# Attention over 26 causal tiles: all early projections first, and the seven shortest tiles set between longer ones

## The chip, the cores and the metric

The kernel runs on one core of a Trainium2 chip. A core has a matrix engine (PE, with its weight loads shown apart as PEld), a vector engine (DVE), a scalar engine (ACT), a general engine (POOL) and a queue engine (SP) that issues transfers here. Each works through its own instructions in the order in which they were written; semaphores join them. The metric is the time of one execution on the device in microseconds (us).

## What is computed

Two layers of a graph network on 3327 nodes with 256 features. Layer 0 is a normalised graph convolution and a mixture of 8 experts, layer 1 a graph attention and a last feed-forward block. Only that last block (`_L1_ffn_ref`) is touched. Cut to what matters:

```python
sx = einsum('bsh,ndh->bnsd', x, hl_w) + hl_b          # x: layer-normed rows; 4 heads of 64
q = einsum('bnsd,neod->bneso', sx, wq)                # 4 experts for each head
k = einsum('bnsd,nod->bnso', sx, wk)
v = einsum('bnsd,nod->bnso', sx, wv)
scores = einsum('bnesd,bntd->bnest', q, k) * d ** 0.5 + causal
att = softmax(scores, axis=-1)
qkv = einsum('bnest,bntd->bnesd', att, v)             # zero where sx is zero
# a softmax gate mixes the 4 experts; + residual; layernorm; two small
# linear layers; layernorm; a softmax gate over the heads; + x
```

The causal mask makes the work of a row grow with its place: row s attends to rows 0 to s.

## The kernel before

`heads` (line 745) does this block. The rows lie in 26 tiles of 128. A unit is a tile t and a head h; its keys are cut into chunks of 512 columns, so that a unit has t // 4 + 1 chunks and the last one has 128, 256, 384 or 512 columns. In all there are 392 chunks, from 4 in each of tiles 0 to 3 up to 28 in tiles 24 and 25.

`prepare(t)` (line 852) makes what a tile needs: it loads the rows `xres` from the DRAM tensor `xs`, normalises them (`pst`, `pmv`, `prs` with a power on POOL, `xn`), turns them on PE (`xt`), projects them (`psxt`, evicted to `sxt`), copies them by four transfers to the layout `sxd`, makes the values (`pv`, `v`, four stores to the DRAM tensor `vs`), the keys (`pk`, into `kt`, which holds the keys of all tiles), the queries (`pq`, `qt`), a zero mask in `sxd` and the turned rows `sx`. It is a Python generator of nine steps: each `yield` lets other work be written in between. `begin(u)` (line 1189) is called when the first chunk of a unit is to be filled. At a tile's head 0 it first runs the open prepare to its end (`while preps: run(preps)`) and then opens that of the next tile; tile 0's runs alone ahead of everything.

A chunk goes through five acts:

- `fill` (944): eight score matmuls into four PSUM banks (`pqk`), and in a unit's last chunk the mask matmuls.
- `drain`: four DVE reads of the banks into one of 9 buffers `sc`, with the running maximum of each row.
- `weigh`: the exponentials on ACT, which need the maximum over all chunks of the unit (`anmax`).
- `turn`: a transpose of `sc` in 32 by 32 blocks on DVE.
- `attend`: the matmuls with the values (`vr`, loaded by `values` from `vs` with four transfers for each chunk) into the sums `po`.

A unit ends with `over` (ACT copies `po` to `ot`, POOL multiplies by the mask) and, one chunk later, `back` (1048: PE turns `ot` back into `ptO`, ACT copies it to `qkv` and `glp`). With a tile's head 3, `back` opens a `tail` (1110): gate, residual, two layernorms, two linear layers, the last gate, the store. A tail is a generator too, of 17 steps, with much of its work on POOL. Before it is opened, `while len(tails) > 2: run(tails)` runs the open tails step by step until at most two are left.

The order is written out in one loop over the chunks. In turn k it drains up to `wanted(k)` (1221) chunks, which is k + 3 plus t // 4 of the tile two chunks ahead, attends to chunk k, turns chunk k + 1, loads and weighs chunk k + 2, and fills one more. One step of every open tail and prepare is run in each turn that does not follow a unit's end; for tiles below 8 in every turn. The class `InOrder` keeps all instructions of an engine in this written order.

The PSUM tiles of `fill`, `prepare`, `back` and `tail` come from one ring of four banks (tag `b`). The buffers that matter below: two of `xres`, `qt`, `qkv`, three of `sxd`, `fx`, `fo`, five of `sx`, one of `v` and `ot`.

Of the kernel before, what the change touches and what calls it, by code (L numbers as in the profile page):

```python
# [11 lines left out]
F32 = mybir.dt.float32  # L12
# [9 lines left out]
P = 128  # L22
# [6 lines left out]
NB = (NP + BLK - 1) // BLK  # L29
NEG = -1e30  # L30


# [68 lines left out]
class Net:  # L101
# [642 lines left out]

    def heads(self, xs, vs, out):
        tc, a = self.tc, self.a
        nc = InOrder(tc)
        Q = 32
        with ExitStack() as ctx:
# [4 lines left out]
            tl = ctx.enter_context(tc.tile_pool(name="att", bufs=2))  # L754
            sm = ctx.enter_context(tc.tile_pool(name="atsm", bufs=4))
            ps_o = ctx.enter_context(tc.tile_pool(name="pso", bufs=1, space=PSUM))
# [94 lines left out]

            def prepare(t, res):

                x = tl.tile([P, D], F32, tag="xres", name="xres", bufs=2)
                nc.sync.dma_start(out=x, in_=xs[ts(t, P), :])
# [9 lines left out]
                yield  # L865
                xn = self.work.tile([P, D], F32, tag="xn", name="xn2", bufs=1)
                nc.vector.tensor_scalar(xn, x, mv[:, 0:1], rs, ALU.subtract, ALU.mult)
                load["dve"] += 0.35
                yield
                xt = self.work.tile([P, 2, P], F32, tag="xt", name="xt2")  # L870
                turned(xn, xt)
                yield
                pp = ps.tile([P, 2, P], F32, tag="b", name="psxt")
                for c in range(2):
                    for k in range(2):
                        nc.tensor.matmul(
                            pp[:, c, :], hlt[:, k, ts(c, P)], xt[:, k, :], start=(k == 0), stop=(k == 1)
                        )
                sxt = self.work.tile([P, 2, P], F32, tag="sxt", name="sxt")
                for c in range(2):  # L880
# [5 lines left out]

                sxd = self.work.tile([P, 4, P], F32, tag="sxd", name="sxd", bufs=3)
                for k in range(2):
# [27 lines left out]
                yield  # L916
                qt = tl.tile([P, 4, 2, P], F32, tag="qt", name="qt")
                pp = [ps.tile([P, 2, 2, P], F32, tag="b", name="pq") for _ in range(2)]
# [12 lines left out]
                load["dve"] += 0.4  # L931
                sx = tl.tile([P, D], F32, tag="sx", name="sx", bufs=5)
                turned(sxt.rearrange("p c q -> p (c q)"), sx.rearrange("p (c q) -> p c q", c=2))
                res.update(sx=sx, sxd=sxd, qt=qt)

            def run(gens):

                gens[:] = [g for g in gens if next(g, None) is None and g.gi_frame is not None]

            tails, preps, ready = [], [], {}  # L940


# [23 lines left out]
            def drain(u, g):  # L966

                n = min(BLK, (u["t"] + 1) * P - g * BLK)
                if g == 0:
                    u["sc"] = {}  # L970
                    u["mx"] = sm.tile([P, 4, 8], F32, tag="mx", name="mx")
                sc = u["sc"][g] = scp.tile([P, 4, BLK], F32, tag="sc", name="sc")
                for e in range(4):
                    nc.vector.tensor_scalar(
                        sc[:, e, :n], u["pq"][e][:, :n], 1.0, None,
                        ALU.mult, ALU.max, accum_out=u["mx"][:, e, g : g + 1],
                    )
                    load["dve"] += 0.12 + 0.00104 * n
                if g == u["t"] // 4:
                    u["nmax"] = sm.tile([P, 4], F32, tag="nmax", name="anmax")  # L980
                    nc.vector.tensor_reduce(
                        u["nmax"], u["mx"][:, :, : g + 1], AX.X, ALU.max, negate=True
                    )
                    load["dve"] += 0.2

            def weigh(u, g, experts):

                n = min(BLK, (u["t"] + 1) * P - g * BLK)
                q = ready[u["t"]]
                if u["h"] == g == 0 and 0 in experts:  # L990
                    q["den"] = sm.tile([P, 16, 7], F32, tag="den", name="aden", bufs=3)
                for k in experts:
                    e = u["sc"][g][:, k, :n]
                    nc.scalar.activation(
                        e, e, AF.Exp, bias=u["nmax"][:, k : k + 1],
                        accum_out=q["den"][:, 4 * u["h"] + k, g : g + 1],
                    )
                    load["act"] += 0.26 + 0.00088 * n
# [49 lines left out]
            def back(u):  # L1048


                h = u["h"]
                r = ready[u["t"]]
                if h == 0:
                    r["qkv"] = tl.tile([P, 4, 4, 64], F32, tag="qkv", name="qkv", bufs=2)
                    r["glp"] = sm.tile([P, 4, 4, 4], F32, tag="glp", name="glp")
                pt = ps.tile([P, 4, 68], F32, tag="b", name="ptO")
                for e in range(4):
                    nc.tensor.matmul(
                        pt[:, e, :], u["ot"][:, e, :], igw[:, h, e, :], start=True, stop=True
                    )  # L1060
                nc.scalar.copy(r["qkv"][:, h, :, :], pt[:, :, :64])
                nc.scalar.copy(r["glp"][:, h, :, :], pt[:, :, 64:])
                load["act"] += 0.55
                if h == 3:
                    while len(tails) > 2:
                        run(tails)
                    tails.append(tail(u["t"], u["sx"], r["qkv"], r["glp"], r["den"]))
# [42 lines left out]
            def tail(t, sx, qkv, glp, den):  # L1110
# [23 lines left out]
                )  # L1134
                fx = tl.tile([P, D], F32, tag="fx", name="fx", bufs=3)
                f3 = fx.rearrange("p (h d) -> p h d", h=4)
# [9 lines left out]
                yield  # L1146
                h1 = tl.tile([P, 2, P], F32, tag="h1", name="h1")
                ph = ps.tile([P, 2, P], F32, tag="b", name="ph1")
# [9 lines left out]
                for c in range(2):  # L1158
                    nc.tensor.matmul(p2[:, ts(c, P)], h1[:, c, :], fc2, start=True, stop=True)
                fo = tl.tile([P, D], F32, tag="fo", name="fo", bufs=3)  # L1160
                nc.vector.tensor_tensor(
# [12 lines left out]
                turned(fo, fot)  # L1174
                x = tl.tile([P, D], F32, tag="xend", name="xend", bufs=2)
                nc.sync.dma_start(out=x, in_=xs[ts(t, P), :])
# [9 lines left out]

            units = [dict(t=t, h=h) for t in range(NT) for h in range(4)]
            chunks = [(u, g) for u in units for g in range(u["t"] // 4 + 1)]
            def begin(u):

                t = u["t"]
                if u["h"] == 0:
                    while preps:
                        run(preps)
                    if t == 0:
                        for _ in prepare(0, ready.setdefault(0, {})):
                            pass
                    if t + 1 < NT:
                        preps.append(prepare(t + 1, ready.setdefault(t + 1, {})))
                u.update(ready[t])  # L1200
# [12 lines left out]
            def drain_to(n):  # L1213
                nonlocal drained
                while drained < min(n, len(chunks)):
# [3 lines left out]
                    drained += 1  # L1219

            def wanted(k):

                return k + 3 + chunks[min(k + 2, len(chunks) - 1)][0]["t"] // 4

# [10 lines left out]
            for k, (u, g) in enumerate(chunks):  # L1235
                ahead = chunks[k + 2] if k + 2 < len(chunks) else None
                drain_to(wanted(k))
                attend(u, g)
                if k + 1 < len(chunks):
                    turn(*chunks[k + 1])  # L1240
                if ahead:
                    values(*ahead)
                    if ahead[1]:
                        weigh(*ahead, range(2))
                if ended:
                    back(ended)
                last = u if g == u["t"] // 4 else None
                if last:
                    over(u)
                if not ended or u["t"] < 8:  # L1250
                    run(tails)
                    run(preps)
                ended = last
                if ahead:
                    weigh(*ahead, range(2 if ahead[1] else 0, 4))
                if filled == drained:
                    fill_next()
# [441 lines left out]
@with_exitstack  # L1699
def tile_adj_ffn_d2(ctx: ExitStack, tc: tile.TileContext, a: dict, out: bass.AP):  # L1700
    net = Net(ctx, tc, a)
    dram = ctx.enter_context(tc.tile_pool(name="dram", bufs=1, space=bass.MemoryType.DRAM))
    xs = dram.tile([NP, D], F32, name="xs")

    vs = dram.tile([4, 7, 32, 16, 64], F32, name="vs")
    with tc.tile_pool(name="feat", bufs=1) as fp:


        net.x = fp.tile([P, NT, D], F32, name="x")
        weights = net.graph1_weights(fp)  # L1710
        with ExitStack() as moe:
            experts = Experts(moe, net, dram, fp)
            net.graph0(experts, weights)
            experts.run()
        net.graph1(xs, experts)
    net.heads(xs, vs, out)

# [77 lines left out]
```

## Time and profile before

| | us |
|---|---|
| median of three runs | 3140.39 (3131.49 to 3145.39) |
| the profiled execution | 3139.96 |
| its span | 3138.3 |
| first score matmul of tile 0 | 999.25 |
| last unit of tile 6 ends | 1282.71 |
| last unit of tile 25 ends | 3100.38 |
| PE busy over the span | 2760.8 (88%) |
| DVE busy over the span | 2495.9 (80%) |
| ACT busy over the span | 1666.3 (53%) |

The profile tells for each engine when it was busy, and for an idle stretch what ended it. Names such as "pqk<-kt,qt" are the written tile and those read. A stretch can be asked for its busy times alone; the column PEclk is the share of the full clock that was granted to PE in it. Matmuls of one engine overlap, so a busy PE is not a PE at its peak. Nearly all instructions carry line 60, that of the helper that records them; names, not lines, tell them apart.

### The profile page before, as it was taken

How to read it: one execution, taken by the hardware profiler on the slowest of the kernel's cores; microseconds unless marked ns; L12 is line 12 of the kernel's file. 1: busy time of each engine (PE TensorE's matmuls, PEld its weight loads, DVE VectorE, ACT ScalarE, POOL GpSimd, SP SyncE). 2: the span in 40 equal slices, each digit the busy share in tenths (PEclk: the TensorE clock that was granted, in tenths of full speed). 3: DMA queues.
4: the chain of work that ended last, by engine and by line, in shares of the span. 5: the costliest groups of instructions: out<-in, count | busy, mean ns of one | idle time of the engine just before them, and what ended most of it. 6: DMA issues, size and time to landing. Idle time of an engine off the chain costs nothing.

```text
span 3138.3 us, 126690 instructions
## 1 busy us (share of the span) xinstructions
PE 2760.8 (88%) x54254; PEld 2025.1 (65%) x54254; DVE 2495.9 (80%) x6166; ACT 1666.3 (53%) x4541; POOL 892.9 (28%) x1216
## 2 busy tenths in 40 slices
PE   7999988798896878989998998899998889999884
PEld 6888877577775656666666665556665556656553
DVE  5104533799994768989999999899999899999994
ACT  6410043755553545656666665566655656565653
POOL 6432554511122453423332222121112111111112
PEclk9999989899997878999999999999999999999997
DMA  9994476777742323334333333343433333333331
GB/s 373 356 272 145 157 232 195 267 249 246 286 168 80 80 59 90 98 85 111 106 99 100 110 104 104 96 107 105 110 102 103 104 104 112 113 104 104 112 104 54
DMA packets 262914, 447.71 MB, mean 143 GB/s; under 512 B 58800, under 2 KB 171696, under 8 KB 262224
## 3 DMA queue, kind: packets, MB, share of 16 engines
q1 hardware_dynamic: 247632, 415.71, 44.0%
q0 software_dynamic: 6960, 19.08, 1.6%
q8 instruction: 428, 7.01, 0.9%
q10 hardware_dynamic: 7760, 4.82, 0.5%
q14 instruction: 134, 1.10, 0.1%
HBM read 406.74 MB, written 25.88 MB: 138 GB/s over the span
## 4 chain that ended last, share of the span: by engine, by line
DVE 39%; PE 25%; issue 3%; ACT 3%; POOL 1%; DMA 1%; ACTq 0%; SPq 0%; POOLq 0%; DVEq 0%
DVE sc L60 34%; PE po L60 10%; PE pqk L60 8%; PE ptO L60 2%; ACT sc L60 2%; PE acc L60 2%; PE pq L60 1%; DVE l2mv L60 0%; PE pt L60 0%; PE psxt L60 0%; DVE l1mv L60 0%; DVE gl L60 0%; PE ph L60 0%; DVE fo L60 0%; DVE l2st L60 0%
## 5 line engine op out<-in xcount | busy, mean ns | idle before, releaser
L60 ACT ACTIVATE sc<-sc,anmax 128x512 f32<-128x512 f32 (+3 forms) x1568 | 1041.4, 671 | 125.2 <-DVE anmax L60 125.2
L60 DVE TENSOR_SCALAR_CACHE_REDUCE sc<-pqk 128x512 f32<-128x512 f32 (+3 forms) x1568 | 898.6, 627 | 111.5 <-PE pqk L60 110.1
L60 PEld LDWEIGHTS po<-sc,vr 32*64 32x64 f32 x43728 | 678.1, 134 | 377.6 <-DVE sc L60 203.6
L60 PE MATMUL po<-sc,vr 32*64 32x128 f32 x43728 | 784.2, 280 | 129.4 <-DVE sc L60 60.2
L60 PE MATMUL pqk<-kt,qt 64*128 64x512 f32 (+3 forms) x3136 | 833.7, 586 | 56.1 <-DVE fo L60 18.9
L60 DVE STREAM_TRANSPOSE sc<-sc 128x2048 f32<-128x2048 f32 (+3 forms) x392 | 815.8, 2082 | 10.9 <-ACT sc L60 10.8
L60 PEld LDWEIGHTS pqk<-kt,qt 64*128 64x128 f32 x3136 | 322.2, 189 | 296.3 <-issue 122.3
L60 PE MATMUL acc<-wh,p 128*128 128x259 f32 x1352 | 309.5, 387 | 34.5 <-DVE p L60 34.5
L60 POOL TENSOR_TENSOR ot<-ot,sxd 128x512 f32<-128x512 f32 x104 | 132.7, 1276 | 695.0 <-ACT ot L60 683.6
L60 PEld LDWEIGHTS acc<-wh,p 128*128 128x128 f32 x1352 | 254.3, 191 | 91.9 <-DVE p L60 52.2
L60 PE MATMUL acc<-y,pan 128*128 128x256 f32 x1352 | 300.7, 382 | 9.3 <-DMA pan<-in_adjt_dram 7.5
L60 ACT ACTIVATION_READ_ACCUMULATOR sc<-sc,anmax 128x1 f32 x1568 | 303.4, 193 | 0.0
L60 PEld LDWEIGHTS acc<-y,pan 128*128 128x128 f32 x1352 | 256.4, 191 | 49.0 <-issue 15.0
L60 ACT ACTIVATE u<-u,d 128x512 f32<-128x512 f32 (+1 forms) x182 | 125.2, 688 | 157.5 <-DVE u L60 157.3
L60 ACT COPY qkv<-ptO 128x256 f32<-128x256 f32 x104 | 38.7, 372 | 278.6 <-PE ptO L60 278.6
L60 DVE SCALAR_TENSOR_TENSOR u<-bc,d 128x512 f32<-128x512 f32 (+1 forms) x182 | 135.3, 744 | 0.1
L60 DVE SCALAR_TENSOR_TENSOR p<-pan,u 128x512 f32<-128x512 f32 (+1 forms) x182 | 125.9, 692 | 10.7 <-PE acc L60 5.8
L60 PE MATMUL ptO<-igw,ot 128*128 128x68 f32 x832 | 118.8, 287 | 12.9 <-DVE sc L60 6.0
L60 DVE DVE_READ_ACCUMULATOR sc<-pqk 128x1 f32 x1568 | 128.6, 82 | 0.0
L60 PEld LDWEIGHTS ptO<-igw,ot 128*128 128x128 f32 x832 | 104.2, 196 | 32.3 <-issue 21.1
L60 ACT ACTIVATE junk<-ar 128x1664 bf16<-128x1664 f32 x52 | 82.7, 1591 | 65.8 <-DMA ar<-in_adj_dram 64.6
L60 POOL TENSOR_TENSOR qkv<-qkv,gss 128x1024 f32<-128x1024 f32 x26 | 50.0, 1924 | 210.1 <-DVE gss L60 210.1
(286 smaller groups left out, 2874.7 us busy)
## 6 DMA issues: line engine op xcount, KB each, us to landing
vr<-vs SPq DMA_DIRECT2D x1248, 128.0 KB
ar<-in_adj_dram SPq DMA_DIRECT2D x104, 832.0 KB
pan<-in_adjt_dram SPq DMA_DIRECT2D x156, 256.0 KB
pan<-in_adjt_dram SPq DMA_DIRECT2D x26, 1024.0 KB
pan<-in_adjt_dram SPq DMA_DIRECT2D x20, 832.0 KB
w1e<-in_w_dram SPq DMA_DIRECT2D x59, 256.0 KB
vr<-vs SPq DMA_DIRECT2D x96, 96.0 KB
took<-places SPq DMA_DIRECT2D x59, 129.0 KB
```

The lines of the kernel that those rows point to most:

```text
L60: made = make(*args, **kw)
```

## The change

The order of the tiles changes from 0, 1, ..., 25 to 7, 8, 9, 0, 10, 11, 1, 12, 13, 2, 14, 15, 3, 16, 17, 4, 18, 19, 5, 20, 21, 6, 22, 23, 24, 25. Tile 7 still needs the keys and values of tiles 0 to 6. So all eight prepares run first, one opened in each round and every open one taken a step further. Their temporaries lie in the buffers `sc`, unused at that time. A tenth step, `keep`, stores `qt`, `sxd` and `sx` of tiles 0 to 6 in a new DRAM tensor `kept`; `fetch` loads them again when the large tile ahead of a small one is begun. The lookahead of `wanted` no longer falls back at a small tile: it takes the largest t // 4 met so far. At most one open tail is left at a tile's end. Some buffers become more (`qt` 3, `sxd` 4, `sx` 6, `mx` and `nmax` 8, `den` 4), others fewer (`xres`, `xt`, `h1`, `xend` 1, `fx`, `fo`, `glp` 2, the small ones 3).

```diff
+FEW = 7
-            def prepare(t, res):
-                x = tl.tile([P, D], F32, tag="xres", name="xres", bufs=2)
+            def prepare(t, res, many=False):
+                if many:
+                    room = scp.tile([P, 4, BLK], F32, tag="sc", name="room")
+                    x, xn = room[:, 0, :D], room[:, 0, D:]
+                    xt, sxt = (room[:, 1, ts(i, D)].rearrange("p (c q) -> p c q", c=2) for i in range(2))
+                else:
+                    x = tl.tile([P, D], F32, tag="xres", name="xres", bufs=1)
...
                 res.update(sx=sx, sxd=sxd, qt=qt)
+                if t < FEW:
+                    yield
+                    keep(t, res)
...
+            order, few = [], deque(range(FEW))
+            for t in range(FEW, NT):
+                order.append(t)
+                if few and t > FEW and (t - FEW) % 2 == 0:
+                    order.append(few.popleft())
+            def keep(t, res):
+                nc.sync.dma_start(out=kept[t, :, ds(0, 1024)], in_=res["qt"].rearrange("p h i q -> p (h i q)"))
+                nc.sync.dma_start(out=kept[t, :, ds(1024, 512)], in_=res["sxd"].rearrange("p h q -> p (h q)"))
+                nc.sync.dma_start(out=kept[t, :, ds(1536, D)], in_=res["sx"])
+            def fetch(t, res):
+                qt = tl.tile([P, 4, 2, P], F32, tag="qt", name="qt", bufs=3)
+                sxd = self.work.tile([P, 4, P], F32, tag="sxd", name="sxd", bufs=4)
+                sx = tl.tile([P, D], F32, tag="sx", name="sx", bufs=6)
+                nc.sync.dma_start(out=qt.rearrange("p h i q -> p (h i q)"), in_=kept[t, :, ds(0, 1024)])
+                nc.sync.dma_start(out=sxd.rearrange("p h q -> p (h q)"), in_=kept[t, :, ds(1024, 512)])
+                nc.sync.dma_start(out=sx, in_=kept[t, :, ds(1536, D)])
+                yield
+                res.update(sx=sx, sxd=sxd, qt=qt)
...
-                    while len(tails) > 2:
+                    while len(tails) > 1:
                         run(tails)
...
-            units = [dict(t=t, h=h) for t in range(NT) for h in range(4)]
+            units = [dict(t=t, h=h) for t in order for h in range(4)]
             def begin(u):
                 t = u["t"]
-                if u["h"] == 0:
+                if u["h"] == 0 and t >= FEW:
                     while preps:
                         run(preps)
-                    if t == 0:
-                        for _ in prepare(0, ready.setdefault(0, {})):
-                            pass
-                    if t + 1 < NT:
-                        preps.append(prepare(t + 1, ready.setdefault(t + 1, {})))
+                    if t == FEW:
+                        coming = deque(range(FEW + 1))
+                        while coming or preps:
+                            if coming:
+                                n = coming.popleft()
+                                preps.append(prepare(n, ready.setdefault(n, {}), many=True))
+                            run(preps)
+                    for n in order[order.index(t) + 1 :]:
+                        ready[n] = {}
+                        preps.append((fetch if n < FEW else prepare)(n, ready[n]))
+                        if n >= FEW:
+                            break
                 u.update(ready[t])
...
+            ahead_of = list(accumulate((u["t"] // 4 for u, _ in chunks), max))
             def wanted(k):
-                return k + 3 + chunks[min(k + 2, len(chunks) - 1)][0]["t"] // 4
+                return k + 3 + ahead_of[min(k + 2, len(chunks) - 1)]
...
-                if not ended or u["t"] < 8:
+                if not ended or u["t"] <= FEW:
                     run(tails)
                     run(preps)
```

More of the change, by code (lines that the diff above doesn't have):

```diff
@@ L2 @@
 from contextlib import ExitStack
-from itertools import chain
+from itertools import accumulate, chain
 import concourse.bass as bass
@@ L742, in graph1, with heads @@
                 finish(t)
-    def heads(self, xs, vs, out):
+    def heads(self, xs, vs, kept, out):
         tc, a = self.tc, self.a
@@ L754, in heads @@
             tl = ctx.enter_context(tc.tile_pool(name="att", bufs=2))
-            sm = ctx.enter_context(tc.tile_pool(name="atsm", bufs=4))
+            sm = ctx.enter_context(tc.tile_pool(name="atsm", bufs=3))
             ps_o = ctx.enter_context(tc.tile_pool(name="pso", bufs=1, space=PSUM))
@@ L847, in turned @@
                 empty(dst, pt, D)
-            def prepare(t, res):
-                x = tl.tile([P, D], F32, tag="xres", name="xres", bufs=2)
+            def prepare(t, res, many=False):
[5 more added lines that the diff above has]
+                    x = tl.tile([P, D], F32, tag="xres", name="xres", bufs=1)
+                    xn = self.work.tile([P, D], F32, tag="xn", name="xn2", bufs=1)
+                    xt = self.work.tile([P, 2, P], F32, tag="xt", name="xt2", bufs=1)
+                    sxt = self.work.tile([P, 2, P], F32, tag="sxt", name="sxt")
                 nc.sync.dma_start(out=x, in_=xs[ts(t, P), :])
@@ L865, in prepare @@
                 yield
-                xn = self.work.tile([P, D], F32, tag="xn", name="xn2", bufs=1)
                 nc.vector.tensor_scalar(xn, x, mv[:, 0:1], rs, ALU.subtract, ALU.mult)
@@ L869, in prepare @@
                 yield
-                xt = self.work.tile([P, 2, P], F32, tag="xt", name="xt2")
                 turned(xn, xt)
@@ L878, in prepare @@
                         )
-                sxt = self.work.tile([P, 2, P], F32, tag="sxt", name="sxt")
                 for c in range(2):
@@ L885, in prepare @@
                 yield
-                sxd = self.work.tile([P, 4, P], F32, tag="sxd", name="sxd", bufs=3)
+                sxd = self.work.tile([P, 4, P], F32, tag="sxd", name="sxd", bufs=4)
                 for k in range(2):
@@ L916, in prepare @@
                 yield
-                qt = tl.tile([P, 4, 2, P], F32, tag="qt", name="qt")
+                qt = tl.tile([P, 4, 2, P], F32, tag="qt", name="qt", bufs=3)
                 pp = [ps.tile([P, 2, 2, P], F32, tag="b", name="pq") for _ in range(2)]
@@ L931, in prepare @@
                 load["dve"] += 0.4
-                sx = tl.tile([P, D], F32, tag="sx", name="sx", bufs=5)
+                sx = tl.tile([P, D], F32, tag="sx", name="sx", bufs=6)
                 turned(sxt.rearrange("p c q -> p (c q)"), sx.rearrange("p (c q) -> p c q", c=2))
                 res.update(sx=sx, sxd=sxd, qt=qt)
+                if t < FEW:
+                    yield
+                    keep(t, res)
             def run(gens):
@@ L940, in heads @@
             tails, preps, ready = [], [], {}
+            order, few = [], deque(range(FEW))
[8 more added lines that the diff above has]
+            def fetch(t, res):
+                qt = tl.tile([P, 4, 2, P], F32, tag="qt", name="qt", bufs=3)
+                sxd = self.work.tile([P, 4, P], F32, tag="sxd", name="sxd", bufs=4)
+                sx = tl.tile([P, D], F32, tag="sx", name="sx", bufs=6)
+                nc.sync.dma_start(out=qt.rearrange("p h i q -> p (h i q)"), in_=kept[t, :, ds(0, 1024)])
[3 more added lines that the diff above has]
+                res.update(sx=sx, sxd=sxd, qt=qt)
             def fill(u, g):
@@ L970, in drain @@
                     u["sc"] = {}
-                    u["mx"] = sm.tile([P, 4, 8], F32, tag="mx", name="mx")
+                    u["mx"] = sm.tile([P, 4, 8], F32, tag="mx", name="mx", bufs=8)
                 sc = u["sc"][g] = scp.tile([P, 4, BLK], F32, tag="sc", name="sc")
@@ L979, in drain @@
                 if g == u["t"] // 4:
-                    u["nmax"] = sm.tile([P, 4], F32, tag="nmax", name="anmax")
+                    u["nmax"] = sm.tile([P, 4], F32, tag="nmax", name="anmax", bufs=8)
                     nc.vector.tensor_reduce(
@@ L990, in weigh @@
                 if u["h"] == g == 0 and 0 in experts:
-                    q["den"] = sm.tile([P, 16, 7], F32, tag="den", name="aden", bufs=3)
+                    q["den"] = sm.tile([P, 16, 7], F32, tag="den", name="aden", bufs=4)
                 for k in experts:
@@ L1054, in back @@
                     r["qkv"] = tl.tile([P, 4, 4, 64], F32, tag="qkv", name="qkv", bufs=2)
-                    r["glp"] = sm.tile([P, 4, 4, 4], F32, tag="glp", name="glp")
+                    r["glp"] = sm.tile([P, 4, 4, 4], F32, tag="glp", name="glp", bufs=2)
                 pt = ps.tile([P, 4, 68], F32, tag="b", name="ptO")
@@ L1134, in tail @@
                 )
-                fx = tl.tile([P, D], F32, tag="fx", name="fx", bufs=3)
+                fx = tl.tile([P, D], F32, tag="fx", name="fx", bufs=2)
                 f3 = fx.rearrange("p (h d) -> p h d", h=4)
@@ L1146, in tail @@
                 yield
-                h1 = tl.tile([P, 2, P], F32, tag="h1", name="h1")
+                h1 = tl.tile([P, 2, P], F32, tag="h1", name="h1", bufs=1)
                 ph = ps.tile([P, 2, P], F32, tag="b", name="ph1")
@@ L1159, in tail @@
                     nc.tensor.matmul(p2[:, ts(c, P)], h1[:, c, :], fc2, start=True, stop=True)
-                fo = tl.tile([P, D], F32, tag="fo", name="fo", bufs=3)
+                fo = tl.tile([P, D], F32, tag="fo", name="fo", bufs=2)
                 nc.vector.tensor_tensor(
@@ L1174, in tail @@
                 turned(fo, fot)
-                x = tl.tile([P, D], F32, tag="xend", name="xend", bufs=2)
+                x = tl.tile([P, D], F32, tag="xend", name="xend", bufs=1)
                 nc.sync.dma_start(out=x, in_=xs[ts(t, P), :])
@@ L1705, in tile_adj_ffn_d2 @@
     vs = dram.tile([4, 7, 32, 16, 64], F32, name="vs")
+    kept = dram.tile([FEW, P, 1024 + 512 + D], F32, name="kept")
     with tc.tile_pool(name="feat", bufs=1) as fp:
@@ L1715, in tile_adj_ffn_d2 @@
         net.graph1(xs, experts)
-    net.heads(xs, vs, out)
+    net.heads(xs, vs, kept, out)
 def _laid_out(i):
```

## The prediction

> **What bounds the kernel now.** I read three views in this order: busy shares by stretch (does a stage have idle time?), the order of time inside the stretch that has it (what is the idle time made of?), and single groups of the moved work (what does that work cost elsewhere?).
>
> First the busy time by stretch. The bounds are starts of "ot<-po" copies on ACT, the last act of a unit (a tile and a head): tile 0's first score matmul starts at 999.25, tile 6 ends at 1282.71, tile 25 at 3100.38. Columns: stretch, length, then busy us of PE, PEld, DVE, ACT, POOL, then the granted clock.
>
> ```profile
> 969.00:999.25 30.25, 11.71 (x60) 9.32 (x58) 4.59 (x14) 3.04 (x9) 11.01 (x49) 0.63 0.28 61
> 999.25:1282.71 283.46, 240.01 (x4456) 177.23 (x4458) 204.18 (x661) 149.15 (x498) 116.47 (x127) 0.85 0.28 76
> 1282.71:1590.68 307.97, 283.61 (x7226) 192.77 (x7222) 286.13 (x751) 188.58 (x581) 99.73 (x110) 0.99 0.36 101
> 1590.68:2591.64 1000.96, 903.34 (x24702) 606.77 (x24702) 928.96 (x2226) 601.00 (x1805) 204.79 (x230) 0.98 0.37 104
> ```
>
> Tiles 12 to 21 (last line) run with DVE 93% and PE 90% busy: two engines nearly full. Tiles 0 to 6 (second line) have DVE at 72%, PE at 85% with a clock of 0.85. That stretch is what the change goes at, 283.5 us. Its parts, tile by tile:
>
> ```profile
> 999.25:1028.04 28.79, 22.44 (x292) 18.61 (x294) 14.88 (x69) 13.20 (x55) 4.31 (x4) 0.74 0.25 62
> 1083.67:1120.61 36.94, 32.22 (x612) 24.39 (x610) 27.73 (x76) 19.77 (x63) 15.30 (x17) 0.86 0.24 63
> 1120.61:1189.61 69.00, 53.40 (x798) 38.20 (x797) 39.55 (x157) 27.64 (x98) 34.52 (x43) 0.70 0.21 57
> 1236.34:1282.71 46.37, 43.07 (x1038) 30.07 (x1040) 43.00 (x119) 29.34 (x91) 19.96 (x22) 1.00 0.37 103
> 1521.98:1590.68 68.70, 63.91 (x1714) 42.91 (x1710) 66.36 (x163) 42.11 (x125) 19.92 (x22) 1.00 0.39 107
> 1590.68:1670.78 80.10, 71.19 (x1872) 48.53 (x1872) 73.56 (x196) 49.05 (x159) 21.87 (x25) 1.00 0.34 96
> ```
>
> These are tiles 0, 3, 4, 6, 11 and 12. Tile 6 is already as full as the large ones (DVE 43.0 of 46.4); tile 4 loses 29 us. What its hole is, the order of time on DVE shows:
>
> ```profile
> 1128.86 0.42 DVE L60 TENSOR_TENSOR fo<-ph,fb 128x256 f32<-128x256 f32 x1 [1.47 <-PE ph L60]
> ...
> 1132.53 0.23 DVE L60 BATCH_NORM_STATS2 l2st<-fo 128x6 f32<-128x64 f32 x1 [2.52 <-POOL fo L60]
> ...
> 1139.76 0.42 DVE L60 TENSOR_TENSOR fo<-ph,fb 128x256 f32<-128x256 f32 x1 [4.52 <-PE ph L60]
> ```
>
> From 1126 to 1143 nothing but steps of tails runs: `back` forces `run(tails)` until few enough are left, so the steps stand one behind another, each waiting for POOL or PE. In those 17.0 us DVE is busy 7.6. Before tiles 1 to 4 the same happens to `prepare`: `begin` forces its last 7, 5, 5 and 5 steps (1009.7 to 1024.6 for tile 1 between two "ot" copies that else lie 3.5 apart).
>
> **The change part by part.** The sum is made on the profiled execution: 3139.96 us, a span of 3138.3 and 1.66 around it; the median of the three runs shown is 3140.39, so both stand for the same.
>
> *Projections of tiles 0 to 7 first.* Until sxt of tile 0 nothing changes: its reciprocal root waits on POOL for the igw copies and masks until 986.76, its first copy on ACT for the constant loads until 991.4, sxd's first DMA issues at 994.61. Then eight prepares run one step apart. PE needs 0.44 (turn), 1.07 (psxt), 0.70 (pv), 0.78 (pk), 0.98 (pq), 0.44 (turn) = 4.4 us for a tile at full clock; for tile 0, at the 0.50 granted from 987 to 999, 0.66 + 2.04 + 1.22 + 1.23 + 1.92 + 0.69 = 7.8. SP issues in this order:
>
> ```profile
> 994.61 2.58 SPq L60 DMA_DIRECT2D sxd<-sxt  x4
> 997.29 1.98 SPq L60 DMA_DIRECT2D vs<-v  x4
> ```
>
> plus xres 0.4 and three stores to `kept`. Those are new and larger (256 to 512 KB by the tile shapes); their issue is bounded by 0.30 (the shortest vr load) and 0.65 (one sxd move) each; I take 0.45, the usual vr load: 1.35. So SP needs 6.3 us a tile, more than a warm PE. From 994.6: 8 x 2.58 + 8 x 1.98 + 5 x 0.4 + stores of tiles 0 to 5, 8.1 = 46.6, so tile 7's scores can start at about 1042 if SP alone sets the pace. If PE stays at half clock: 991.8 + 8 x 7.8 = 1054. Waits on top: v has one buffer, so ACT or DVE wait each time for the vs stores to land, and qt's three and sxd's four buffers wait for stores just issued; xres from issue (969.27) to its reader (971.48) took 2.2, and 2.2 x 3 exposed makes the upper end 1061. Below 1042 nothing can go, as the queue's issues are all counted. I take 1048, nearest to the SP sum because most of the latencies lie beside other tiles' steps. Against 999.25: **+49**.
>
> The clock decides part of this. In the rows, "psxt" takes 421 ns in tiles 0 to 6 and 276 from 1400 to 2900, and PE had 0.63 granted from 1010 to 1024 while 74% busy. [...]
>
> *Start of tile 7.* `wanted(0)` drains four chunks before the first `attend`: a fill (2.28) and four drains of four 0.61 us reads with a wait for the next fill (about 0.5) is 14; then transpose 2.31, po 2.09 and the second chunk's, 21 in all. Now tile 7's first "ot" comes 1293.85 - 1282.71 = 11.1 after tile 6's end. **+10**.
>
> *Tiles 7 to 25.* Same work and nearly the same lookahead: 3138.3 - 1293.85 = 1844.5 kept, **0**. Forced steps of prepare: tiles 8 to 12 had one each; now tile 8 has 4 and tile 9 one: even.
>
> *Tiles 0 to 6 between large ones.* Cost of a chunk among large tiles, from the tile table: a chunk of 128 columns more in each of four units costs 80.1 - 68.7 = 11.4 (12 against 11), 12.3 (16 to 15), 13.1 (20 to 19), 7.9 (24 to 23), mean 11.2; 256 columns 12.5; 384 columns 11.8; 512 columns (15 less 11, 19 less 15, 23 less 19) 23.8, 16.1, 17.3, mean 19.1. The rest of tiles 11, 15, 19 and 23 over their full chunks is 11.4, 16.1, 13.1, 11.3, mean 13.0 (tail, prepare, four units' ends); without prepare (1.5 on DVE, 4.4 on PE) about 10. Tiles 0 to 3: 11.2 + 12.5 + 11.8 + 19.1 = 54.6; tiles 4 to 6: 57.3 + 35.5 = 92.8; ends 70: 217. Low end: their DVE work, 204.2 less some 14 for seven projections (1.5 each and a share of the emptying of kt and qt), at 0.945: 201. High end: this stretch as it is without the forced runs and two hidden prepares, 283.5 - 55 - 8 = 220, and 8 more if the mix binds PE and DVE by turns, 228. I take 217, whose rows are the same kinds of chunks in the same company. **-66.5**. So the mixing itself gains little: a small chunk's step is short on DVE but fills, attends and goes back on PE.
>
> *Tails.* At most one may be left when a tile ends (two before), and a small tile gives a tail only four runs of its 17. By the counts of runs, tile 0's end forces 4 steps, tile 1's 5, and tiles 9, 10, 2, 3 one each: 13, against the 5 of now, whose cost is inside the 283.5. A forced step cost (17.0 - 7.6) / 5 = 1.9 net: **+24** (0 if all is hidden; 44 at 3.4 each). While they run, chunks behind them on PE and DVE stand still.
>
> *Fetches.* Three loads for a tile (7 x 3 x 0.45 = 9.5 us of SP) issued when the large tile before is begun, that is twelve chunks or more ahead of their use; SP is little used there (1.8 of 5 us a chunk). Buffers of qt and sxd come round with all readers done. **0**; they cost up to their landing, 2.2 a tile, if a large tile's chunks ran out. Fewer buffers for fx, fo, h1, xend: two tails at a time need no more, 0.
>
> Sum: 49 + 10 - 66.5 + 24 = +16.5: 3139.96 + 16.5, rounded **3157** (0.5% over the median).
>
> **The rivals.**
> *Faster.* The dense mix takes the small tiles at their bare work, 201, forced steps are hidden by the chunks drained ahead (0), SP alone paces the start (+43): 43 + 10 - 82.5 = -29.5, 3110. For it: tiles 22 and 23 run DVE at 98 and 97%. Against: each fourth tile, whose last chunks are small, falls to 88 to 92% (12, 16, 20). It decides below -16, which needs both the bare work and no forced cost.
> *A draw.* As forecast, but forced steps at half price (12) and a start at 1043: +44 + 10 - 66.5 + 12 = 0, 3140.
> *A slow front.* In-order waits make a round of the projections 10 us (v's store and landing 2.0 + 2.2, then sxd 2.6, and the stores): 8 x 3.7 = 30 more, 3187. For it: in tiles 0 to 6 DVE waited 14.7 for "kt" and 17.0 for sxd's move. Against: eight tiles are in flight.
> *No effect*, the code being inert, is excluded: order and projections do change.
>
> **How the numbers follow.** About 0.5% (16 us) is what a measurement of this kernel can tell from no change. Forecast 0.42 (3145 to 3172, two thirds of it above the bound), slow front 0.17, draw 0.17, faster 0.24. Faster by over 0.5% is 0.24; slower: 0.28 + 0.17 = 0.45; within: 0.14 + 0.17 = 0.31. The range, 3112 to 3192, leaves out the ends of the faster and slow-front cases; the forecast's own is 3145 to 3172.
>
> **What would show it.** The first "pqk" of tile 7 between 1042 and 1061, with SP filled from 994 on; its first "ot" 21 later; a large tile with its small one at 28 to 40 us over the same large tile alone; holes of some 10 us on DVE and PE, behind "fo" and "fx" of POOL, soon after tiles 0 and 1 end; from tile 22 on each tile as long as now. It is wrong if small tiles cost under 200 together, or the start comes after 1065.

## The result

The changed kernel takes 3160.98 us in the median of five runs (3156.37 to 3165.85), the kernel before 3139.66 beside it: a ratio of 1.0074 with a 95% interval of 1.0051 to 1.0097, so 21 us slower. The profiled execution took 3165.85, with a span of 3164.1.

First the busy times by stretch of the changed kernel, columns as before. The stretches are: up to tile 7's first score matmul (1048.20), from there to the end of its first unit ("ot<-po", 1069.22), to tile 25's last unit, and the rest.

```profile
969.00:1048.20 79.20, 46.70 (x342) 39.33 (x340) 22.57 (x67) 20.02 (x55) 15.08 (x56) 0.77 0.48 129
1048.20:1069.22 21.02, 18.73 (x302) 10.92 (x302) 18.65 (x46) 10.08 (x29) 0.00 (x0) 0.90 0.65 193
1069.22:3125.64 2056.42, 1832.51 (x49340) 1246.36 (x49340) 1859.45 (x4605) 1218.96 (x3704) 494.01 (x546) 0.97 0.37 103
3125.64:3164.10 38.46, 6.65 (x24) 5.01 (x24) 6.71 (x35) 2.67 (x8) 15.26 (x18) 0.53 0.01 4
```

The same stretch of the kernel before, from tile 7's first unit to tile 25's last:

```profile
1293.85:3100.38 1806.53, 1629.45 (x45188) 1097.88 (x45188) 1678.86 (x4004) 1092.81 (x3272) 379.88 (x423) 0.99 0.37 105
```

To the first score 999.25 became 1048.20 (+49.0). From there to tile 7's first unit 294.6 became 21.0. From that unit to tile 25's last 1806.5 became 2056.4: with the seven small tiles and their forced tail steps in it, it is 249.9 longer. The rest grew by 0.5. Together 49.0 - 273.6 + 249.9 + 0.5 = 25.8, the difference of the two spans.

Two places carry this. In the projections SP's queue is seldom idle: from 995.88 to 1048.20 its issues take 47.0 of the 52.3 us (order of time on SP, changed kernel; columns start, length, transfer):

```profile
1015.04 0.46 SPq L61 DMA_DIRECT2D kept<-qt  x1
1015.94 0.34 SPq L61 DMA_DIRECT2D kept<-sxd  x1
1016.38 0.47 SPq L61 DMA_DIRECT2D kept<-sx  x1
1016.95 2.08 SPq L61 DMA_DIRECT2D vs<-v  x4
1019.29 2.56 SPq L61 DMA_DIRECT2D sxd<-room  x4
1021.89 0.59 SPq L61 DMA_DIRECT2D kept<-qt  x1
```

That is one round of a tile, 6.85 us from one store of `qt` to the next. And after small tiles come holes. Busy times of tile 0, of tile 10's first unit after it, and of the rest of tile 10:

```profile
1231.05:1252.44 21.39, 17.67 (x211) 11.35 (x212) 18.16 (x66) 13.12 (x51) 10.62 (x12) 0.92 0.33 97
1252.44:1278.83 26.39, 19.98 (x410) 14.03 (x411) 18.00 (x53) 11.19 (x37) 11.51 (x13) 0.81 0.21 58
1278.83:1324.53 45.70, 42.83 (x1180) 28.59 (x1180) 44.89 (x115) 29.90 (x92) 17.22 (x19) 1.00 0.46 129
```

Tile 10's first unit takes 26.4 with DVE 68% busy, where the other three take 15.2 on average with DVE at 98%. The order of time on PE inside it:

```profile
1259.30 1.11 PE L61 MATMUL ptO<-igw,ot 128*128 128x68 f32 x8 [2.24 <-POOL ot L61]
1260.24 0.38 PE L61 MATMUL pt<-ident,fo 128*128 128x128 f32 x2
1261.22 1.01 PE L61 MATMUL pfg<-fgw,fot 128*128 128x4 f32 x4 [0.59 <-ACT fot L61]
1265.10 0.69 PE L61 MATMUL pt<-ident,fx 128*128 128x128 f32 x2 [2.87 <-POOL fx L61]
1266.25 1.23 PE L61 MATMUL ph<-fxt,fc 128*128 128x128 f32 x4 [0.46 <-ACT fxt L61]
```

Only steps of tails run from 1260 to 1267: the last steps of tile 8's and steps of tile 9's, forced by `back` at the end of tile 0.

### The profile page after: what moved, and what is told of

It reads as the page before. It is cut to its first block, busy times and chain, and to the rows that moved or that the text cites. A ratio compares the mean times of both kernels' runs of the same rounds, so it can differ in the third digit from the quotient of the medians.

```text
span 3164.1 us, 126793 instructions
## 1 busy us (share of the span) xinstructions
PE 2768.1 (87%) x54254; PEld 2029.9 (64%) x54254; DVE 2497.8 (79%) x6177; ACT 1662.5 (53%) x4530; POOL 895.5 (28%) x1216
## 4 chain that ended last, share of the span: by engine, by line
DVE 36%; PE 23%; ACT 4%; issue 2%; POOL 1%; DMA 1%; SPq 0%; POOLq 0%; DVEq 0%; ACTq 0%
DVE sc L61 32%; PE po L61 10%; PE pqk L61 8%; ACT sc L61 3%; PE ptO L61 2%; DVE l2mv L61 1%; PE ph L61 1%; PE pq L61 0%; DVE l1mv L61 0%; PE pt L61 0%; DMA vr<-vs 0%; DVE fo L61 0%; DVE l2st L61 0%; POOL fx L61 0%; PE psxt L61 0%
## 5 line engine op out<-in xcount | busy, mean ns | idle before, releaser
L61 PEld LDWEIGHTS acc<-wh,p 128*128 128x128 f32 x1352 | 253.8, 190 | 92.3 <-DVE p L61 51.9
L61 PEld LDWEIGHTS ptO<-igw,ot 128*128 128x128 f32 x832 | 105.6, 199 | 39.9 <-issue 22.5
L61 DVE CUSTOM_DVE_ANT_0 sg<-sg,dst 128x1664 bf16<-128x1664 bf16 (+2 forms) x56 | 99.7, 1788 | 4.0 <-ACT dst L61 4.0
```

The source lines that it names most:

```text
L61: made = make(*args, **kw)
```

## The experiments

The runs were made in several sessions. In two of them the stages ahead of `heads` end some 20 us sooner, and the kernel before takes 3121 to 3122 there instead of 3138 to 3140. So each time is compared with the kernel before of the same session, and inside a trace times are counted from the first transfer of sxd or from the first score. Values in brackets behind a ratio are its 95% interval.

### Are the forced steps of tails dear? (a_tails2)

```diff
-                    while len(tails) > 1:
+                    while len(tails) > 2:
                         run(tails)
```

> The changed kernel with two open tails allowed at a tile's end instead of one. By the count of generator steps no step of a tail is then forced (13 before). Theory (the prediction's sum: forced steps cost about 24 us, of which some 20 are to be seen as the long first units of tiles 10 and 12): the time falls by 15 to 24, to 3137 to 3146, and the first units of tiles 10 and 12 take 15 to 22 us instead of 26 and 30. Rival (the mix of small and large chunks is itself dear, the holes after tiles 0 and 1 would come in any case): less than 5 us gained, 3156 or more.

Measured: 3139.14, kernel before 3121.25, ratio 1.0056 (1.0037 to 1.0076). Busy times of the first units of tiles 10 and 12 in this kernel:

```profile
1230.06:1245.98 15.92, 13.89 (x389) 10.05 (x386) 15.34 (x48) 9.86 (x32) 9.05 (x13) 1.00 0.33 90
1387.93:1409.24 21.31, 18.70 (x476) 13.19 (x476) 20.09 (x63) 12.66 (x43) 10.20 (x14) 1.00 0.38 100
```

The holes are gone as expected (15.9 and 21.3 instead of 26.4 and 30.4), but the time is not: from tile 7's first unit to tile 25's last it is 2043.7. Tile 10 as a whole takes 68.3 where the changed kernel took 72.1, tile 12 takes 84.4 instead of 93.0: the steps that are no longer forced run inside those tiles and take time there. The theory has the mechanism and not its size.

The changed kernel itself was run again (after_again):

> The changed kernel itself, on the same chip as the next two runs. 0.5 to 1.0% slower than the kernel before, as measured first.

It gave 3142.01 against 3122.42, ratio 1.0072 (1.0046 to 1.0098). And the first variant once more, in more runs:

> The changed kernel with two open tails allowed, again, beside the next one on the same chip. The traces so far let the 13 forced tail steps cost at most 12 us where the prediction had 24 (the holes after tiles 0 and 1 go, 20 us, but tiles 10 and 12 as wholes shrink by 4 and 6). Theory (most of the work of a forced step only moves): 0.4 to 0.6% slower than before the change, 2 to 10 us below the changed kernel. Rival (24 us as predicted): no slower than before the change.

3152.98 against 3138.45, 1.0037 (1.0022 to 1.0053). From 1.0072 and 1.0074 to 1.0056 and 1.0037 is 0.16 to 0.37%, 5 to 12 us: the theory, and half or less of the 24 that the prediction had. The four intervals overlap in part; with each pair pooled, the difference is 9 us with an interval of some 2 to 16, so neither nothing nor 24. The changed kernel's own second profile gave 2040.6 for the stretch that took 2056.4 in the first, no more than the two profiles without forced steps (2043.7 and 2040.7), so single profiles can't settle a term of this size.

### Does the order matter? (b_order, b_order_t3)

Projections first as in the change, attention from 0 to 25:

```diff
-            order, few = [], deque(range(FEW))
-            for t in range(FEW, NT):
-                order.append(t)
-                if few and t > FEW and (t - FEW) % 2 == 0:
-                    order.append(few.popleft())
+            order = list(range(NT))
...
-                    while len(tails) > 1:
+                    while len(tails) > 2:
                         run(tails)
...
-                        coming = deque(range(FEW + 1))
+                        coming = deque([*range(1, FEW + 1), 0])
...
```

> Projections of tiles 0 to 7 first, as in the changed kernel, but attention in the order 0 to 25 (tile 0 is projected last of the eight, tiles 1 to 7 are stored and fetched; two open tails allowed, as before the change). Theory (the start costs 49, the mixing itself gains nothing over the same tiles in a row without forced prepares): first scores at about 1048, tiles 0 to 6 in 238 us from there (283.5 less 37 of forced prepares less 8 of prepares run beside the work), so 3143 in all, 18 below the changed kernel and even with the one before. Rival (small tiles run better between large ones, only the start is dear): tiles 0 to 6 take 255 or more and the time is 3160 or more.

Measured: 3137.48 against 3121.25, ratio 1.0048 (1.0031 to 1.0065). From the first score to tile 6's end it took 243 us (1032.0 to 1274.8), near the 238 of the theory; the start cost 47 (first score 52.0 after the first sxd transfer, 4.7 in the kernel before). Still it ended 15 us over the kernel before, where the theory had it even: its other tiles took 5 more and its forced tail steps after tile 3 are in it. So neither the theory nor the rival: the order is not where the 21 us are, at least not alone. With three open tails nothing is forced there (b_order_t3, `while len(tails) > 3`):

> Projections of tiles 0 to 7 first, attention in the order 0 to 25, three open tails allowed, so that neither a prepare nor a tail is forced there: against the run before it on this chip it differs by the order alone. Theory (small tiles between large ones cost more than in a row, since a small chunk still fills, attends and goes back on PE beside a large one): even with the kernel before the change within 6 us, 10 to 20 us below the changed kernel with two tails. Rival (mixing costs nothing by itself): within 5 us of the changed kernel with two tails.

3135.13 against 3138.45, ratio 0.9991 (0.9979 to 1.0003). Against the mixed order without forced steps (1.0037 and 1.0056) that is 14 to 20 us less, as the theory had it. From the first score to the last unit the mixed order takes 2061.9 and 2065.2, this one:

```profile
1048.80:3092.01 2043.21, 1833.00 (x49640) 1246.22 (x49640) 1883.97 (x4650) 1228.45 (x3733) 495.23 (x546) 0.98 0.38 106
```

Half of the 19 to 22 us between them is tile 7, with which the mixed order starts: it takes 60.7 and 62.2 instead of 50.6, since nothing runs ahead of its first unit (21 us to its end, 11 in the kernel before). Tiles 0 to 6 take 230 instead of 228, and tiles 8 to 25 take 1774.4 and 1770.1 instead of 1764.3. But the kernels that have the order 0 to 25 in common differ as much among themselves in tiles 8 to 25 (1762.0 to 1772.1). So a cost of the mixing itself, some 7 to 12 us here, is not shown; what is shown is that it gains nothing.

Five forced tail steps in the order 0 to 25 cost (1.0048 - 0.9991) x 3140 = 18 us, give or take 7: more than the 13 forced steps among large tiles.

### What sets the length of the start? (c_keep_pool, d_rooms, g_front_free)

In the first, `keep` issues its three stores from POOL's queue (first pair of lines); in the second, v and qt of tiles 0 to 6 lie in free parts of the `room` buffers (the rest); the third has both:

```diff
-                nc.sync.dma_start(out=kept[t, :, ds(1536, D)], in_=res["sx"])
+                nc.gpsimd.dma_start(out=kept[t, :, ds(1536, D)], in_=res["sx"])
...
+                if many:
+                    v = room[:, 0, :D].rearrange("p (h d) -> p h d", h=4)
...
+                if many and t < FEW:
+                    qt = room[:, 2:4, :].rearrange("p a (h i q) -> p (a h) i q", h=2, i=2)
...
```

> The changed kernel with the three stores of each kept tile issued from POOL's queue instead of SP's. Theory (SP's queue paces the projections: 21 of its 71 issues from 995.9 to 1052 are these stores, some 12 us): tile 7's first score matmul comes at 1038 to 1041 instead of 1048.2. Rival (the pace is set by waits for the landing of stores, v's above all: ACT and DVE waited 24 us for it, qt's 12): the first score comes within 3 us of 1048.

> The changed kernel with v and qt of tiles 0 to 6 in buffers of their own (unused parts of the temporaries' buffers), so that no eviction waits for a store to land. Theory (SP's queue paces the projections, those waits lie beside its issues): tile 7's first score matmul stays within 3 us of 1048.2. Rival (the landings set the pace): it comes 6 us or more sooner.

> The changed kernel with both: v and qt of tiles 0 to 6 in buffers of their own and the stores of kept tiles issued from POOL's queue. Counted from the first transfer of sxd, the changed kernel's first score matmul came after 52.3 and tile 7's first end of a unit after 73.3 (with the queue alone relieved 47.9 and 67.8, with the buffers alone 42.7 and 70.1). Theory (the queue holds back the projections and then the first loads of vr, which stand behind the stores): first scores after 36 to 41, first unit after 57 to 62. Rival (each of them is only one of several limits of the same length, DVE's waits for sxd among them): first unit after 65 or later.

Counted from the first transfer of sxd, in one profile each:

| | first score | end of tile 7's first unit |
|---|---|---|
| changed kernel | 52.3 | 73.3 |
| stores from POOL's queue (c) | 47.9 | 67.8 |
| buffers of their own (d) | 42.7 | 70.1 |
| both (g) | 47.2 | 72.9 |

Four profiles of kernels that share the start of the changed kernel (two of it, two with two open tails) give 51.9 to 53.1 and 73.1 to 74.7, so differences of 2 us and more mean something here. The whole times, of one run each, are 3135.93 (c) and 3143.38 (d) against 3121.25, and 3164.53 (g) against 3138.45: 15, 22 and 26 us over the kernel before. Runs of one kernel spread by up to 26, so nothing more is read from them.

Stores from another queue bring the first score 4.4 sooner, where the theory had 7 to 10 and the rival at most 3; buffers bring the first score 9.6 sooner, against the theory, but the first unit only 3.2, because its first loads of vr stand behind the stores in SP's queue (issued 56 us after the first sxd transfer, as in the changed kernel). Both together gain nothing. The order of time on SP in that kernel:

```profile
1014.92 2.56 SPq L61 DMA_DIRECT2D sxd<-room  x4
1017.58 4.44 SPq L61 DMA_DIRECT2D vs<-room  x4
1022.82 5.52 SPq L61 DMA_DIRECT2D sxd<-room  x4
1028.44 4.03 SPq L61 DMA_DIRECT2D vs<-room  x4
1032.58 2.55 SPq L61 DMA_DIRECT2D sxd<-room  x4
```

With the stores gone from it the queue's own transfers take up to twice as long to issue (5.5 and 4.4 against 2.6 and 2.0), and DVE waits 22.1 us for sxd to land (20.9 in d). The rival holds: there are several limits of nearly one length, and relieving one shows the next. The longer issues come with the stores' move to POOL's queue: in the seven profiles with the stores on SP's queue the 64 transfers of sxd and vs take 34.4 to 35.3 us to issue together, with the stores on POOL's queue 39.9 (c) and 45.4 (g). By what way, no run shows.

### Are the holes before tiles 1 to 4 work, or the latency of forced steps? (e_two_ahead, e_two_ahead_t3)

This takes nothing of the change but its buffer counts: order 0 to 25, no projections ahead, no DRAM. The next two tiles are projected at a time (`start(n)` opens the prepare of tile n), and `begin` only forces what tile t itself needs. The edit, against the kernel before:

```diff
                 if u["h"] == 0:
-                    while preps:
-                        run(preps)
                     if t == 0:
-                        for _ in prepare(0, ready.setdefault(0, {})):
-                            pass
+                        start(0)
+                    while any(g in preps for g in opened[: t + 1]):
+                        run(preps)
+                        if t == 0 and len(opened) < 2:
+                            start(1)
-                    if t + 1 < NT:
-                        preps.append(prepare(t + 1, ready.setdefault(t + 1, {})))
+                    while len(opened) < min(NT, t + (3 if t <= FEW else 2)):
+                        start(len(opened))
```

> Nothing of the change but its buffers: order 0 to 25, no projections ahead, no stores to DRAM, two open tails; tile 1 is projected beside tile 0, and up to tile 7 the prepare of the tile after next is opened too, so that the counts of forced prepare steps fall from 31 after tile 0 (7, 5, 5, 5, 2 before tiles 1 to 5) to 7 (3 before tile 2). Theory (the holes before tiles 1 to 4 are the latency of forced steps, not work): 25 to 37 us less than the kernel before (0.8 to 1.2%), the first units of tiles 1, 3 and 4 without holes but for the forced tail. Rival (the small tiles are bound by PE and DVE work whatever the order of the steps): less than 10 us gained.

3087.32 against 3122.42: ratio 0.9884 (0.9853 to 0.9915), 35 us faster. The theory. With three open tails as well:

> As the kernel with prepares two tiles ahead, with three open tails at a tile's end, so that the five forced tail steps after tile 3 go. Theory: 10 to 17 us less than that kernel, the first unit of tile 4 at some 10 us instead of 23. Rival (what the forced steps do has to wait for POOL anyway, later): less than 4 us.

3068.94 against 3122.42: 0.9829 (0.9804 to 0.9854), 53 us faster, 18 of it from the tails, a little over the theory. Busy times of this kernel from the first score to tile 6's end, and of tile 4 (69.0 in the kernel before):

```profile
983.60:1215.38 231.78, 213.96 (x4462) 159.55 (x4460) 204.18 (x660) 148.74 (x500) 116.45 (x127) 0.98 0.35 93
1080.12:1126.29 46.17, 42.71 (x830) 31.88 (x828) 39.68 (x146) 28.59 (x100) 29.43 (x36) 0.96 0.32 84
```

The stretch that took 283.5 takes 231.8, with seven projections in it as before (now of tiles 2 to 8), with DVE at 88% instead of 72 and the granted clock at 0.98 instead of 0.85. So nearly the whole gain of 53 lies there, and this kernel beats both others. The kernel before with the new buffer counts alone was not run; tiles 8 to 25 take 1762 to 1772 us with them and 1765 without, so they change nothing there, but a share of theirs in tiles 0 to 6 is not excluded. The same stretch of the kernel with the projections first and nothing forced (b_order_t3):

```profile
1048.80:1277.11 228.31, 199.78 (x4176) 145.93 (x4178) 192.22 (x620) 128.24 (x441) 111.92 (x120) 0.90 0.39 114
```

The difference, 3.5 us, and 4 more at the start (first score 8.4 after the first sxd transfer instead of 4.7) are what the projections cost on the way, beside other work: some 7 us. Ahead of everything they cost 47 to 49.

## Why the prediction was right

It said 3157 and slower (3145 to 3172 for the forecast); measured were 3160.98. By its steps:

- *Projections first, +49:* right in size, 1048.20 against the 1048 taken. Of its reasons only half: SP's queue was nearly full, at 6.85 us a round where 6.3 were counted, but the runs c, d and g show that buffers and landings limit it just as much. Its floor of 1042 is none: with buffers of their own the first score came 42.6 after the first sxd transfer, which is 1037 counted from 994.61. The sum counts the stores of six tiles ahead of tile 7, and in the changed kernel only those of five stood ahead of the first score. The clock went most of the way to full: 0.83 was granted over the projections (995.88 to 1048.20), against 0.63 from 1010 to 1024 before, and "psxt" took 296 ns in the median of the eight tiles, against 276 from 1400 to 2900 (0.99 granted) and 421 in tiles 0 to 6 before. But the granted clock also fell to 0.50, three times for 3.4 us (from 1004.72, 1021.79 and 1028.61) and once more from 1042.27 to past the first score; the longest gap of PE between 995.88 and the last of these falls was 2.5 us. The start came midway between the two sums, 1042 and 1054, and no run shows that the clock set it.
- *Start of tile 7, +10:* right; first unit 21.0 after the first score, as summed.
- *Tiles 7 to 25, 0, and small tiles 217, -66.5:* mis-sized by some 20. Without forced steps the stretch from tile 7's first unit takes 2043.7 and 2040.7 (both runs with two tails) against 1806.5, so 234 to 237, above even the upper end of 228 that was given. In the first of them the small tiles' own stretches are 230, and tiles 8 to 25 take 9 more, which is within what they differ by from kernel to kernel. Most of the miss is in the price of the small tiles themselves and not in their company: in a row, with nothing projected or forced between them, they take 228.3 (b_order_t3). That the marginal cost of a chunk leaves out what a unit's end costs when nearly every chunk is a last one is a likely reason, but was not tested.
- *Tails, +24:* the mechanism right, holes after tiles 0 and 1 at the places named, behind POOL. Its size was 5 to 12: most of the work in a forced step moves elsewhere when it isn't forced. The price of 1.9 a step came from a place with small tiles around it. There the five steps cost 18, so 3.6 each, by two pairs of runs (b_order and b_order_t3, and the two kernels with prepares two ahead); among large tiles 13 steps cost 0.4 to 0.9 each. The price was right at neither place.
- *Fetches and fewer buffers, 0:* nothing in the trace speaks against it; not tried apart.

The sizes of the small tiles and of the tails miss in opposite directions, by about 20 and 15. That they nearly cancel, so that the sum came out 4 us off, is luck. What carries the verdict holds: the change pays 49 + 10 us ahead, and the small tiles give back 46 to 49 of it (234 to 237 against 283.5), less what the forced tail steps cost.

The rivals: the faster one needed small tiles at 201 and free forced steps; the small tiles took 234 to 237. The draw needed half the price of the forced steps, which came, and the small tiles at 217 and a start at 1043, which did not. The slow front did not come.

Why the change does not gain is the same from the other side. By the ratios, the order 0 to 25 with nothing forced stands at 0.983; projecting first instead of on the way adds 51 us, give or take 9 (0.9829 to 0.9991), the mixed order 14 to 20, its forced tail steps 5 to 12. The traces of the first two kernels show 41 of the 51: the first score comes 43 later after the first sxd transfer, tiles 0 to 6 take 3.5 less and tiles 7 to 25 take 1.5 more.

## What to carry to other kernels

A stretch with idle engines is not yet a stretch that wants other work: look at what fills its holes. Here they were steps of two pipelines forced one behind another, and giving each pipeline one tile more of time gained 53 us with the order untouched, while moving the work ahead paid for its whole latency where nothing ran beside it. And a hole seen in a trace need not be worth its length, since what is forced in it has to be done in any case. Among large tiles, holes with 20 us to be seen gave back 5 to 12. Among the small tiles, with DVE busy 72%, holes priced at 35 to 54 gave back 53. That the free time of the other engines makes this difference is argued, not tested.

## What the runs showed that was not expected

Two reliefs of the same stretch, worth 5.5 and 3.2 us alone at the first unit's end, were worth 0.4 together. Five forced tail steps cost 18 us among small tiles and thirteen 5 to 12 among large ones. Two profiles of the same kernel differ by 16 us over 2050 (2056.4 and 2040.6), so that terms of ten need the timed runs, not the trace.
